# Batch 1's first layer norm as pieces in the queue of keys and values

## The chip, the cores and the metric

The kernel runs on one core of a Trainium2 chip. The core has TensorE (PE; its weight loads are listed as PEld), VectorE (DVE), ScalarE (ACT), GpSimd (POOL) and SyncE (SP), which issues the DMA transfers. Each engine works through its own queue in order, and semaphores tie the queues together. The metric is the device time of one execution in microseconds (us); the figure for a kernel is the median of several runs.

## The reference

The input x has 2 batches of 512 tokens with 512 features, in float32. Four layers are added to x in turn, each of them on a layer norm of x without weights:

```
x = x + attn_a(layernorm(x))   # 32 query heads of 128, 8 key/value heads, causal softmax, rotary positions
x = x + ffn(layernorm(x))      # softmax gate, the best 2 of 8 experts, rank 64
x = x + attn_b(layernorm(x))   # 32 query heads of 16, 8 key/value heads, causal softmax, rotary positions
x = x + ffn(layernorm(x))
```

In attn_a the four weight matrices are stored as integer codes from 0 to 15 with a scale for each group of 128 input rows and each column: w = (code - 8) * scale. The change concerns the very first layer norm, that of attn_a:

```
m = mean(x); v = var(x); (x - m) / sqrt(v + 1e-5)
```

## The kernel before, in words

Everything is tiled to 128 partitions. A batch is NT = 4 tiles of 128 tokens, and the features are NC = 4 chunks of 128.

**The first layer norm.** `two_parts(b)` (L330) does it for batch b through `norm_transposed` (L95). For each of 4 token tiles VectorE takes statistics (L101, L102); ScalarE takes one square root (L104) and VectorE one reciprocal (L106) for all four. Then, tile by tile, VectorE normalizes in place (L110), TensorE transposes the four 128x128 blocks into a PSUM bank (L115, tile pxT_a), and `halves` (L149) splits the result into two parts for the matmuls: ScalarE copies it, rounded, to xh (L151), and VectorE writes the remainder to xl (L152). Both batches are normalized one after the other in the program, batch 0 at L339 and batch 1 at L345, with the loads of the rotary table, of the v scales and of the v codes between them. The scales of the output weights follow (L347). The rows of x lie in two slots of a pool (tag "pT") that the attention later uses for its transposed probabilities.

**Projections.** A head's keys, values or queries are four stages c = 0 to 3 (`projected`, L353). In each, PE multiplies one 128-row chunk of the weights with xh and then with xl into a PSUM bank (L358, L359, tiles ps_k, ps_v, ps_q; two banks, tag "mm"). The first is scaled into SBUF by ScalarE (L363), the other three are scaled and added by VectorE (L365). Keys and queries are then rotated (`rotated`, L369): two VectorE products (L374, L375) and two POOL operations (L376, L377), which write kT or qT. Values are transposed by PE and copied back (L385, L386).

**The attention.** The work is cut into 64 units, one for each of 8 key/value groups g, 2 batches b and 4 heads h, in this order. In step n of the loop at L502, unit n gets its queries, unit n-2 its scores and softmax (L396 matmul, L399 maximum, L404 exponential, L413 division), unit n-3 its weighted values (transposes L424, copies L425, matmuls L429, tile av), and unit n-4 its share of the output projection (L438, L439). These stages are generators, and `in_turn` (L451) takes one piece from each in rotation.

**The queue of keys and values.** Keys and values are made by a further generator, `keys_values(g)` (L476), which for batch 0 and then batch 1 yields 5 pieces for the keys (four stages and the rotation) and 5 for the values. `more` chains those generators over g. Before the loop, 5 pieces are taken (L499), which are the keys of group 0, batch 0. In each step, `some(more, 3 + ...)` (L533) takes 4 pieces while the step's unit is of group 0 (steps 0 to 7), and 3 later. The keys of a unit are read by its softmax two steps after its queries, its values by the weighted values three steps after.

**The order on the engines.** The program's order is a priority, not the order in the queues: an instruction that is ready may be put ahead of earlier ones that are not. The load of the gate weights (L537), which the program issues in step 60 of the loop, stands on SP's queue at 20.86 us.

Of the kernel before, what the change touches and what calls it, by code (L numbers as in the profile page):

```python
# [11 lines left out]
F32 = mybir.dt.float32  # L12
I32 = mybir.dt.int32
F32R = mybir.dt.float32r
AF = mybir.ActivationFunctionType
ALU = mybir.AluOpType
# [3 lines left out]
P = 128  # L20
B, S, DM = 2, 512, 512
NT = S // P
NC = DM // P
# [17 lines left out]
def kernel(  # L41
# [21 lines left out]
    nc = tc.nc  # L63
# [3 lines left out]
    small = ctx.enter_context(tc.tile_pool(name="small", bufs=4))  # L67


    x = {}  # L70
# [7 lines left out]
    ident = const.tile([P, P], F32, tag="ident", name="ident")  # L78
# [7 lines left out]
    eps = const.tile([P, 1], F32, tag="eps", name="eps")  # L86
# [4 lines left out]
    order = const.tile([P, NE], F32, tag="order", name="order")  # L91
    for e in range(NE):
        nc.gpsimd.memset(order[:, e : e + 1], float(NE - e))

    def norm_transposed(b, which, pool, tag, take=None):  # L95


        var = small.tile([P, NT, 2], F32, tag="mv", name=f"mv_{which}_{b}")
        for t in range(NT):
            st = small.tile([P, 6], F32, tag="st", name=f"st_{which}_{b}_{t}")  # L100
            nc.vector.bn_stats(st, x[b, t])  # L101
            nc.vector.bn_aggr(var[:, t, :], st)  # L102
        std = small.tile([P, NT], F32, tag="std", name=f"std_{which}_{b}")
        nc.scalar.activation(std, var[:, :, 1], AF.Sqrt, bias=eps)  # L104
        rstd = small.tile([P, NT], F32, tag="rstd", name=f"rstd_{which}_{b}")
        nc.vector.reciprocal(rstd, std)  # L106
        xT = None if take else xtp.tile([P, NC, S], F32, tag="xnT", name=f"xnT_{which}_{b}")
        for t in range(NT):
            xn = x[b, t] if take else lnp.tile([P, DM], F32, tag="xn", name=f"xn_{which}_{b}_{t}")
            nc.vector.tensor_scalar(  # L110
                xn, x[b, t], var[:, t, 0:1], rstd[:, t : t + 1], ALU.subtract, ALU.mult
            )
            pt = pool.tile([P, NC, P], F32, tag=tag, name=f"pxT_{which}_{b}_{t}")
            for c in range(NC):
                nc.tensor.transpose(pt[:, c, :], xn[:, ts(c, P)], ident)  # L115
            if take:
                take(t, pt)
            else:
                nc.scalar.copy(xT[:, :, ts(t, P)], pt)
        return xT  # L120


    homes, banks, lora = {}, [], {}
# [25 lines left out]
    def halves(src, hi, lo):  # L149

        nc.scalar.copy(hi, src)  # L151
        nc.vector.tensor_tensor(lo, src, hi.bitcast(F32), ALU.subtract)  # L152
# [127 lines left out]
    with ExitStack() as actx:  # L280
# [12 lines left out]
        ps_tp = actx.enter_context(tc.tile_pool(name="ps_tp", bufs=2, space=PSUM))  # L293
# [14 lines left out]
        def whole(codes, u, what, pool=wpool, gpsimd=False):  # L308

            cd = big.tile([P, NC * U], I32, tag="big", name=f"codes_{what}_{u}")  # L310
            nc.sync.dma_start(cd, codes[u])
            w = pool.tile([P, NC, U], F32R, tag="w", name=f"w_{what}_{u}")
            wf = w.rearrange("p c n -> p (c n)")
            if gpsimd:
                nc.gpsimd.tensor_scalar(wf, cd, -8.0, 1.0, ALU.add, ALU.mult)
            else:
                nc.scalar.activation(wf, cd, AF.Copy, bias=-8.0)
            return w

        wkv, xh, xl, own = {}, {}, {}, {}  # L320
# [8 lines left out]

        def two_parts(b):  # L330

            xh[b] = xp.tile([P, NC, S], F32R, tag=f"xh{b}", name=f"xh_{b}")
            xl[b] = xp.tile([P, NC, S], F32R, tag=f"xl{b}", name=f"xl_{b}")
            norm_transposed(
                b, "a", ps_tp, "tp",
                lambda t, pt: halves(pt, xh[b][:, :, ts(t, P)], xl[b][:, :, ts(t, P)]),
            )

        two_parts(0)  # L339

        tab = tabs.tile([P, 2, S], F32, tag="tab", name="tab")
        nc.sync.dma_start(tab, rope_a)
        own["v"] = own_scales(v_scales, 2 * 4 * NC, "v")
        wkv["v"] = whole(v_codes, 0, "v", wkvp, gpsimd=True)
        two_parts(1)  # L345

        so = own_scales(o_scales, A_NH * NC, "o")  # L347

# [20 lines left out]
        def rotated(dst, kind, w, u, h, b, nm):  # L369


            r = yield from projected(kind, w, u, h, b, nm)
            rs = rp.tile([P, S], F32, tag=f"rs{kind}", name=f"rs_{nm}")
            nc.vector.tensor_tensor(rs[0:64], r[64:128], tab[64:128, 1, :], ALU.mult)  # L374
            nc.vector.tensor_tensor(rs[64:128], r[0:64], tab[0:64, 1, :], ALU.mult)  # L375
            nc.gpsimd.tensor_tensor(r, r, tab[:, 0, :], ALU.mult)  # L376
            nc.gpsimd.tensor_tensor(dst, r, rs, ALU.add)  # L377
            yield

        def values_of(dst, w, u, h, b, nm):  # L380

            r = yield from projected("v", w, u, h, b, nm)
            tp = ps_tp.tile([P, NT, P], F32, tag="tp", name=f"tp_{nm}")
            for t in range(NT):
                nc.tensor.transpose(tp[:, t, :], r[:, ts(t, P)], ident)  # L385
            nc.scalar.copy(dst, tp)  # L386
            yield
# [88 lines left out]
        def keys_values(g):  # L476

            u, h = divmod(g, 4)
            if g == 4:
                wkv["k"] = whole(k_codes, u, "k", wkvp)  # L480
                wkv["v"] = whole(v_codes, u, "v", wkvp)
            for b in range(B):
                kTs[g, b] = kvp.tile([P, S], F32, tag="kT", name=f"kT_{g}_{b}")
                vs[g, b] = kvp.tile([P, NT, P], F32, tag="v", name=f"v_{g}_{b}")
                yield from rotated(kTs[g, b], "k", wkv["k"], u, h, b, f"k_{g}_{b}")
                yield from values_of(vs[g, b], wkv["v"], u, h, b, f"v_{g}_{b}")
# [9 lines left out]


        more = keys_values(0)
        in_turn(some(more, 5))  # L499
        units = [(g, b, h) for g in range(A_NKV) for b in range(B) for h in range(A_G)]  # L500
        wo, qTs, prs, ats = {}, {}, {}, {}
        for n in range(len(units) + 4):  # L502
            turn = []

            def at(lag):
                if 0 <= n - lag < len(units):
                    g, b, h = units[n - lag]
                    return (g, b, h, f"{g}_{b}_{h}")

            if at(3):  # L510
                g, b, h, nm = at(3)
# [4 lines left out]
            if at(0):  # L516
                g, b, h, nm = at(0)
                if (b, h) == (0, 0):
                    if g:
                        wq[g] = whole(q_codes, g, "q")  # L520
                    wo[g] = whole(o_codes, g, "o")
                    after = keys_values(g + 1) if g + 1 < A_NKV else iter(())
                    more = chain(more, after)
                qTs[g, b, h] = qtp.tile([P, S], F32, tag="qT", name=f"qT_{nm}")
                turn.append(rotated(qTs[g, b, h], "q", wq[g], g, h, b, f"q_{nm}"))
            if at(4):
                g, b, h, nm = at(4)
                turn.append(output(wo[g], h, g * A_G + h, b, *ats.pop((g, b, h)), nm))
            if at(2):
                g, b, h, nm = at(2)  # L530
# [19 lines left out]
    xtp = ctx.enter_context(tc.tile_pool(name="xnT", bufs=2))  # L550
# [511 lines left out]
```

## Time and profile before

| | |
|---|---|
| median of 3 runs | 1117.19 us (1116.21 to 1117.54) |
| the profiled execution | 1118.06 us, its span 1116.3 us |
| PE busy | 1060.7 us, 4940 matmuls |
| DVE busy | 880.8 us, 2195 instructions |
| ACT busy | 617.4 us, 1421 instructions |
| POOL busy | 587.4 us, 920 instructions |
| L365, scaled sums of the queries | 192 instructions, 747 ns each |
| L115, transposes of the norm, in the first 60 us | 32 instructions, 7.6 us |
| L110, normalizations | 8 instructions, 529 to 1111 ns |

The span is the time from the first to the last instruction of the profiled execution. The page cuts it into 40 slices of 27.9 us and gives for each engine a digit, the busy share in tenths. Other views list the busy time of the engines in any stretch, the chain of work that ended last (each piece led to by what released it), the instructions in order of time, and for one line of the kernel the least, median and longest duration. All times count from the start of the span.

### The profile page before, as it was taken

To read this page: it belongs to the slowest core of one execution; us is meant where nothing else is said; L and a number is where in the kernel's file an instruction comes from. 1 tells how busy PE (TensorE), PEld (TensorE's weight loads), DVE (VectorE), ACT (ScalarE), POOL (GpSimd) and SP (SyncE) were. 2 spreads that over 40 slices of the span, in tenths; PEclk is the share of its full clock that TensorE was granted. 3 is DMA by queue.
4 is the path that set the end of the run, shared out by engine and by line. 5 is a ranking of instruction groups with operands and counts; after the bars stand their busy time and mean duration, and the time that the engine had idled before them with its cause. 6 is when DMAs were issued, how large, how long until landed. Compare 5 with 4: busy or idle time off the path is not lost.

```text
span 1116.3 us, 16200 instructions
## 1 busy us (share of the span) xinstructions
PE 1060.7 (95%) x4940; PEld 708.8 (63%) x4940; DVE 880.8 (79%) x2195; ACT 617.4 (55%) x1421; POOL 587.4 (53%) x920
## 2 busy tenths in 40 slices
PE   5799999999999999999999999999989989999988
PEld 3467677777777777777777777546457555555543
DVE  6889899999999999999999889574376677877252
ACT  3556566577566566566565665513157566585410
POOL 2557566666656656756756666261245566454200
PEclk9999999999999999999999999999989999999999
DMA  7301011022010010010021000042342235111000
GB/s 288 114 1 38 1 38 38 1 76 68 9 39 24 15 38 14 26 38 8 32 76 38 1 1 1 1 156 63 91 156 77 61 106 152 44 44 26 10 33 38
DMA packets 21030, 58.11 MB, mean 52 GB/s; under 512 B 3152, under 2 KB 4112, under 8 KB 18128
## 3 DMA queue, kind: packets, MB, share of 16 engines
q1 hardware_dynamic: 20944, 57.08, 15.6%
q8 instruction: 40, 0.66, 0.2%
q14 instruction: 46, 0.38, 0.1%
HBM read 43.30 MB, written 12.58 MB: 50 GB/s over the span
## 4 chain that ended last, share of the span: by engine, by line
PE 80%; DVE 10%; ACT 3%; POOL 3%; issue 2%; DMA 1%; SPq 0%; ACTq 0%; DVEq 0%; POOLq 0%
PE av L429 11%; PE sc L396 11%; PE tp L424 5%; PE ps_o L439 5%; PE ps_o L438 5%; PE ps_q L358 5%; PE ph_f L207 5%; PE ps_q L359 5%; PE num_b L831 3%; PE st_b L805 3%; PE py_f L266 3%; PE sc_b L758 3%; PE pq_b L678 2%; PE po L885 2%; DVE r_q L365 2%
## 5 line engine op out<-in xcount | busy, mean ns | idle before, releaser
L404 ACT ACTIVATE p<-sc,nmx 128x128 f32<-128x128 f32 (+3 forms) x256 | 135.7, 530 | 95.1 <-DVE nmx L399 92.1
L376 POOL TENSOR_TENSOR r_q<-r_q,tab 128x512 f32<-128x512 f32 x64 | 82.5, 1289 | 190.2 <-DVE rs_q L375 190.2
L396 PE MATMUL sc<-kT,qT 128*128 128x128 f32 (+3 forms) x512 | 180.0, 433 | 1.2 <-POOL qT L377 0.9
L365 DVE SCALAR_TENSOR_TENSOR r_q<-ps_q,s_q,r_q 128x512 f32<-128x512 f32 x192 | 143.4, 747 | 36.1 <-PE ps_q L359 22.4
L413 POOL TENSOR_SCALAR p<-p,rden 128x128 f32<-128x128 f32 (+3 forms) x256 | 140.3, 562 | 58.5 <-DVE rden L411 24.5
L425 ACT COPY pT<-tp 128x128 f32<-128x128 f32 (+3 forms) x256 | 109.4, 428 | 104.1 <-PE tp L424 103.5
L762 DVE CUSTOM_DVE_ANT_0 sc_b<-sc_b,tri 128x128 f32<-128x128 f32 (+3 forms) x256 | 119.6, 516 | 47.3 <-PE sc_b L758 42.5
L429 PE MATMUL av<-pT,v 128*128 128x512 f32 (+3 forms) x512 | 148.5, 433 | 0.0
L429 PEld LDWEIGHTS av<-pT,v 128*128 128x128 f32 x512 | 97.0, 190 | 80.2 <-issue 53.9
L448 DVE SCALAR_TENSOR_TENSOR acc<-ps_o,s_o,acc 128x512 f32<-128x512 f32 x186 | 137.3, 738 | 5.5 <-PE ps_o L439 5.4
L399 DVE CUSTOM_DVE_ANT_0 sc<-sc,tri 128x128 f32<-128x128 f32 (+3 forms) x256 | 125.1, 489 | 8.1 <-PE sc L396 7.3
L358 PE MATMUL ps_q<-xh,w_q 128*128 128x512 f32 x256 | 122.7, 479 | 7.6 <-DVE r_q L365 7.6
L424 PE MATMUL tp<-ident,p 128*128 128x128 f32 x640 | 112.9, 272 | 2.6 <-POOL p L413 2.6
L396 PEld LDWEIGHTS sc<-kT,qT 128*128 128x128 f32 x512 | 95.6, 189 | 25.3 <-ACT p L404 2.0
L438 PE MATMUL ps_o<-ah,w_o 128*128 128x512 f32 x256 | 107.9, 422 | 1.7 <-DVE acc L448 1.0
L811 ACT ACTIVATE pT_b<-st_b 128x384 f32<-128x384 f32 (+1 forms) x192 | 90.1, 528 | 34.4 <-PE st_b L805 33.5
L439 PE MATMUL ps_o<-al,w_o 128*128 128x512 f32 x256 | 104.8, 410 | 3.5 <-DVE al L152 3.5
L424 PEld LDWEIGHTS tp<-ident,p 128*128 128x128 f32 x640 | 83.0, 141 | 30.7 <-issue 6.4
L359 PE MATMUL ps_q<-xl,w_q 128*128 128x512 f32 x256 | 101.2, 395 | 0.0
L814 POOL TENSOR_SCALAR_AFFINE_SELECT pT_b<-pT_b 128x128 f32<-128x128 f32 (+1 forms) x192 | 62.2, 333 | 64.7 <-ACT pT_b L811 62.2
L377 POOL TENSOR_TENSOR qT<-r_q,rs_q 128x512 f32<-128x512 f32 x64 | 85.5, 1335 | 1.0
L446 POOL TENSOR_TENSOR acc<-acc,part 128x512 f32<-128x512 f32 x62 | 79.9, 1288 | 10.2 <-ACT part L445 10.1
(182 smaller groups left out, 2065.4 us busy)
## 6 DMA issues: line engine op xcount, KB each, us to landing
codes_q<-in_q_codes_dram SPq DMA_DIRECT2D x8, 1024.0 KB
codes_o<-in_o_codes_dram SPq DMA_DIRECT2D x8, 1024.0 KB
spread_q<-hl SPq DMA_DIRECT2D x16, 512.0 KB
qs<-spread_q SPq DMA_DIRECT2D x32, 256.0 KB
x_a<-in_x_dram SPq DMA_DIRECT2D x8, 256.0 KB
codes_k<-in_k_codes_dram SPq DMA_DIRECT2D x2, 1024.0 KB
codes_v<-in_v_codes_dram SPq DMA_DIRECT2D x2, 1024.0 KB
x_r<-in_x_dram SPq DMA_DIRECT2D x8, 256.0 KB
```

The costliest lines, as they stand in the source:

```text
L358: nc.tensor.matmul(ps, w[:, c, ts(h, A_HD)], xh[b][:, c, :], start=True, stop=False)
L359: nc.tensor.matmul(ps, w[:, c, ts(h, A_HD)], xl[b][:, c, :], start=False, stop=True)
L365: nc.vector.scalar_tensor_tensor(r, ps, s, r, ALU.mult, ALU.add)
L396: nc.tensor.matmul(sc[:, :n], qT[:, ts(i, P)], kT[:, :n], start=True, stop=True)
L399: nc.vector.tensor_tensor_reduce(sc[:, :n], sc[:, :n], tri[:, S - n :], -(A_HD**-0.5), 3e38, ALU.add, ALU.min, nmx,)
L404: nc.scalar.activation(pr, sc[:, :n], AF.Exp, bias=nmx, scale=-1.0, accum_out=den[:, i % 2 : i % 2 + 1],)
L413: nc.gpsimd.tensor_scalar(prs[j], prs[j], rden[:, j % 2 : j % 2 + 1], 1.0, ALU.mult, ALU.mult)
L424: nc.tensor.transpose(tp[:, j, :], prs[i][:, ts(j, P)], ident)
L429: nc.tensor.matmul(av[:, j * P :], v[:, j, :], pT[:, j, j * P :], start=(j == 0), stop=(j == NT - 1))
L438: nc.tensor.matmul(ps, w[:, h, ts(n, P)], ah, start=True, stop=False)
L439: nc.tensor.matmul(ps, w[:, h, ts(n, P)], al, start=False, stop=True)
L448: nc.vector.scalar_tensor_tensor(to, ps, s, to, ALU.mult, ALU.add)
```

## The change

`norm_transposed` is gone; its body stands in `two_parts`, which is now a generator with five pieces: the statistics of the four tiles with square root and reciprocal, and then one piece for each tile. For batch 0 the generator is run to its end in the old place. For batch 1 it is taken as part of `keys_values(0)`, after the values of batch 0 and ahead of the keys of batch 1. So `more` begins with keys of batch 0 (pieces 1 to 5), values of batch 0 (6 to 10), the norm of batch 1 (11 to 15), keys of batch 1 (16 to 20), values of batch 1 (21 to 25), where the last two were pieces 11 to 15 and 16 to 20. How many pieces a step takes is as before. The instructions, their operands, the pools and the number of buffers are the same.

```diff
-    def norm_transposed(b, which, pool, tag, take=None):
...
         def two_parts(b):
+
             xh[b] = xp.tile([P, NC, S], F32R, tag=f"xh{b}", name=f"xh_{b}")
             xl[b] = xp.tile([P, NC, S], F32R, tag=f"xl{b}", name=f"xl_{b}")
-            norm_transposed(
-                b, "a", ps_tp, "tp",
-                lambda t, pt: halves(pt, xh[b][:, :, ts(t, P)], xl[b][:, :, ts(t, P)]),
-            )
-
-        two_parts(0)
+            var = small.tile([P, NT, 2], F32, tag="mv", name=f"mv_a_{b}")
+            for t in range(NT):
+                st = small.tile([P, 6], F32, tag="st", name=f"st_a_{b}_{t}")
+                nc.vector.bn_stats(st, x[b, t])
+                nc.vector.bn_aggr(var[:, t, :], st)
+            std = small.tile([P, NT], F32, tag="std", name=f"std_a_{b}")
+            nc.scalar.activation(std, var[:, :, 1], AF.Sqrt, bias=eps)
+            rstd = small.tile([P, NT], F32, tag="rstd", name=f"rstd_a_{b}")
+            nc.vector.reciprocal(rstd, std)
+            yield
+            for t in range(NT):
+                xn = x[b, t]
+                nc.vector.tensor_scalar(
+                    xn, xn, var[:, t, 0:1], rstd[:, t : t + 1], ALU.subtract, ALU.mult
+                )
+                pt = ps_tp.tile([P, NC, P], F32, tag="tp", name=f"pxT_a_{b}_{t}")
+                for c in range(NC):
+                    nc.tensor.transpose(pt[:, c, :], xn[:, ts(c, P)], ident)
+                halves(pt, xh[b][:, :, ts(t, P)], xl[b][:, :, ts(t, P)])
+                yield
+
+        for _ in two_parts(0):
+            pass
 
         tab = tabs.tile([P, 2, S], F32, tag="tab", name="tab")
         nc.sync.dma_start(tab, rope_a)
         own["v"] = own_scales(v_scales, 2 * 4 * NC, "v")
         wkv["v"] = whole(v_codes, 0, "v", wkvp, gpsimd=True)
-        two_parts(1)
 
         so = own_scales(o_scales, A_NH * NC, "o")
...
             for b in range(B):
+                if (g, b) == (0, 1):
+                    yield from two_parts(1)
                 kTs[g, b] = kvp.tile([P, S], F32, tag="kT", name=f"kT_{g}_{b}")
```

More of the change, by code (lines that the diff above doesn't have):

```diff
@@ L93 @@
         nc.gpsimd.memset(order[:, e : e + 1], float(NE - e))
-    def norm_transposed(b, which, pool, tag, take=None):
[L98 to L111, printed above, removed]
-            )
[L113 to L120, printed above, removed]
     homes, banks, lora = {}, [], {}
@@ L333, in two_parts @@
             xl[b] = xp.tile([P, NC, S], F32R, tag=f"xl{b}", name=f"xl_{b}")
-            norm_transposed(
-                b, "a", ps_tp, "tp",
-                lambda t, pt: halves(pt, xh[b][:, :, ts(t, P)], xl[b][:, :, ts(t, P)]),
-            )
-        two_parts(0)
+            var = small.tile([P, NT, 2], F32, tag="mv", name=f"mv_a_{b}")
[20 more added lines that the diff above has]
+            pass
         tab = tabs.tile([P, 2, S], F32, tag="tab", name="tab")
```

## The prediction

> **What bounds the kernel now.** I read the page first (busy time, the 40 slices), then stretches of 4 us over the start, then the chain of waits from 17 to 39 us, then the order of VectorE's instructions there.
>
> ```profile
> PE 1060.7 (95%) x4940; PEld 708.8 (63%) x4940; DVE 880.8 (79%) x2195; ACT 617.4 (55%) x1421; POOL 587.4 (53%) x920
> ...
> PE   5799999999999999999999999999989989999988
> ...
> DVE  6889899999999999999999889574376677877252
> ```
>
> TensorE (PE) is busy 95% of the span, and the digits say where it is not: the first two slices, 0 to 56 us. Between 100 and 580 us PE is busy 473.33 of 480.00 us, so a start that is shorter by some time ends the kernel earlier by that time, less the PE work that it left for later. The start itself, by stretches:
>
> ```profile
> core 0: us, PE busy (x) PEld busy (x) DVE busy (x) ACT busy (x) POOL busy (x), PEclk, DMA share, GB/s
> ...
> 24.00:28.00 4.00, 3.87 (x19) 2.96 (x18) 3.44 (x7) 2.54 (x5) 0.00 (x0) 1.00 0.24 70
> 28.00:32.00 4.00, 2.34 (x8) 1.05 (x8) 3.80 (x6) 3.90 (x3) 2.57 (x2) 1.00 0.19 37
> 32.00:36.00 4.00, 3.30 (x14) 1.58 (x12) 3.50 (x6) 2.00 (x3) 0.67 (x1) 1.00 0.99 408
> 36.00:40.00 4.00, 2.58 (x10) 1.57 (x10) 2.39 (x7) 3.81 (x7) 1.87 (x2) 1.00 0.68 236
> ...
> 44.00:48.00 4.00, 2.12 (x9) 1.05 (x9) 3.92 (x7) 0.95 (x2) 3.92 (x5) 1.00 0.00 0
> ```
>
> Here VectorE (DVE) is the fuller engine, except from 36 to 40 us, where it waits for the first rotated queries. From 22.00 to 58.25 us (58.25 is the first weighted-values matmul, av L429) PE is busy 29.01 of 36.25 us and DVE 32.37: 7.24 us of PE time lie idle, 3.88 us of DVE time. The chain of waits (start, length, what) runs through the moved layer norm:
>
> ```profile
> 23.23 1.71 PE pxT_a L115 x8
> ...
> 25.58 1.03 PE pxT_a L115 x4
> 26.64 0.60 ACT xh L151
> ...
> 27.26 0.69 DVE xl L152
> ...
> 27.96 0.69 DVE rs_k L375
> ...
> 28.68 0.69 DVE xl L152
> ...
> 36.68 1.28 POOL qT L377
> ...
> 38.00 0.94 PE sc L396 x4
> ```
>
> All pxT_a, xh and xl after 22 us are batch 1's: 1.71 + 1.03 + 0.60 + 0.69 + 0.69 = 4.72 us of the chain to the first scores at 38.00. None of it is wanted by these scores, which are batch 0's.
>
> **The change part by part.** It adds and removes no instruction. Batch 1's norm is 4 pairs of statistics (0.67 + 0.18 us each), one square root, one reciprocal, 4 normalizations L110, 16 transposes L115, 4 xh copies (0.59) and 4 xl (0.69). It issues no DMA (batch 1's rows are loaded at 4.56 us as before), so SP's queue is passed by nothing, and POOL's neither.
>
> The order on the engines is not the program's (a load that the program issues in step 60, L537, is on SP's queue at 20.86 us). Before, three pairs of statistics stand between 14.86 and 17.05 us, while VectorE has little else that could run. I expect them to stay there, and so the square root at 19.79, ahead of the table load for the first Exp at 37.57: cost zero. If they go later instead, the xl at 17.05 gains about 0.5 us (its xh is there at 16.5), and 4 x 0.85 = 3.4 us fall into fuller time; if the square root lands behind the first Exp, ScalarE reloads twice, 2 x 1.28 = 2.6 us on an engine busy 20.23 of 36.25 us. Bounds: 0.5 gained, 2.6 lost; I take zero, by the nearest row, the gap itself.
>
> What changes is from 21.87 us on:
>
> ```profile
> 21.87 1.91 DVE L110 TENSOR_SCALAR x_a<-x_a,mv_a,rstd_a 128x512 f32<-128x512 f32 x4
> 23.70 0.75 DVE L365 SCALAR_TENSOR_TENSOR r_k<-ps_k,s_k,r_k 128x512 f32<-128x512 f32 x1
> ```
>
> The reader is to see that the last sum of batch 0's keys (23.70; its matmuls end at 22.02) stands behind four normalizations. With these later in priority: r_k at 22.05 to 22.8, its two rs_k (0.69 each) to 24.2. ps_q c0 stays at 22.02; ps_v c0 follows at 22.85 in the bank that r_k frees; ScalarE scales them at 23.3 and 24.0 (0.69 each). ps_q c1 then runs 24.0 to 24.85, and the first of the six L365 for q and v starts at 25.1 rather than 29.29. The six take 4.54 us before (29.29 to 33.83), so they end at about 29.65; rs_q 1.39 and POOL's two with their gaps 2.7 us give first scores at 33.8, against 38.00: 4.2 us. The norm's remains (4 L110, 1.91; 4 xl, 2.76) slip into VectorE's gaps in between, and one L110 too many in front of a waiting L365 costs about 0.5. **First scores 3.7 us earlier**, and, if the steps after it keep their distance, av at 54.5. VectorE's own ledger agrees: by then it has not done batch 1's v (3 L365, 2.25 us), and filling half of its 3.88 idle us gives 1.9: 4.2 us.
>
> Given back: the queue of key/value pieces is five behind. At four a step, batch 1's keys end in step 3 (before: 2), its values in step 4 (before: 3); they are wanted by softmax in step 6 and by the weighted values in step 7, so nothing starves. But batch 1's v (8 matmuls at 0.23 and 4 transposes 0.44 together, by the chain's rows near 56 us) is then PE work in time that PE bounds: 2.3 us. Net **1.4 us, the lower end**.
>
> The upper end is PE's ledger. In the stretch above, PE's idle time from 28 to 32 (1.66) and 36 to 40 us (1.42) is behind the moved work or lacks filler, which the norm now is; that from 44 to 48 (1.88) waits for POOL's probabilities and stays. With both gone 3.1 us. Beyond, 12 of the moved transposes take 1.71 + 1.03 = 2.74 us in the chain, where later groups of four (L424) take 0.44: 1.4 us saved if they run at that later pace. Together 4.5 us. Between 1.4 and 4.5 I take the middle, **3.0 us**, since half of PE's idle time has the norm in front of it in the chain.
>
> Covers: the slot of x_a of batch 1 is wanted by pT of unit 1, first written at 61.19; the norm is done some 20 us earlier. PSUM's two "tp" banks: tp_v ends before 35 us and the first tp of the weighted values is at 46.80, so the transposes find one free; without that cover they wait for one xl, 0.7 us. The transposes of the output scales (L303, 0.42; copy 0.28) pass ahead of the norm; they overtake nothing on the chain but 0.3 us.
>
> [...] The matmul pairs at 21.17 and 21.59 stand 0.43 us apart, those at 48.12 and 48.35 0.23, while the granted clock reads 1.00 in all these stretches: the pace changes near 26 us. [...]
>
> ```profile
> L110 DVE TENSOR_SCALAR x_a<-x_a,mv_a,rstd_a x8: 529/538/1111, 10.5 to 23.2; 128x512 f32<-128x512 f32 x8
> ```
>
> Least, median and longest of L110: the 1111 ns one stands beside POOL's L315 (from 9.39 to 11.29). [...] By the rows alone: 0 to 4 x 0.57 = 2.3 us lost on VectorE; I take 0.5, which is in the sum above.
>
> **Rivals.**
> 1. It washes out, or the order hardly changes. The pieces are ready early, so the norm may be put where it was; or the 2.3 us beside POOL cancel the 1.4 to 3.0. For it: the statistics fill gaps whatever their priority. Against it: at 22.05 a ready L365 has priority now. 1115.0 to 1119.4.
> 2. Slower: a late norm holds PE's queue. Before, the first matmul of batch 1's keys (34.84) comes 5.5 us after the last xl (29.37). Now pieces 15 and 16 are neighbours, and a ps_k that stands in PE's queue ahead of its xl stops everything behind it: L110 0.5 + transposes 0.45 + xh 0.6 + xl 0.7 = 2.3 us, and 1.9 more if a weight conversion (L317, 1.92, three of them from 28 to 37 us) is on ScalarE ahead of xh: 4.2. Less the 1.4 that is sure, 2.8 us slower: 1120.0. It decides once PE waits over some 3.5 us at these lines. Against it: the order puts ready work first.
> 3. A larger gain: all of 4.5, the 0.5 of the statistics, and PE's 1.41 idle us from 72 to 76 (two rs_q of 1.15 and 1.68 beside POOL) drawn apart by the shift: 6.4, so 1110.8.
>
> **How the numbers follow.** The rows are of an execution of 1118.06 us (span 1116.3, 1.8 around it). 1118.06 - 3.0 = 1115.06; that execution is 0.87 above the median of the runs, 1117.19, so I predict 1114.2. Forecast (1.4 to 4.5 faster: 1112.7 to 1115.8) 0.54; washed out or unchanged 0.17; slower 0.23; larger gain 0.06. Over 0.2% (2.2 us, about what a measurement tells from no change) faster: 0.43 of the forecast and the larger gain, 0.49. Within: the forecast's 0.11 and 0.15 of the wash-out, 0.26. Slower: 0.23 and 0.02, 0.25. The range, 1111.0 to 1121.0, takes in the slower rival and leaves out most of the larger gain and stalls that come twice.
>
> **What would show it.** Right: r_k's last L365 near 22 us, first sc near 34 (33 to 35), av near 54.5, batch 1's xl between 26 and 38 us, PE idle from 28 to 40 us down from 3.8 to under 2 us, and PE idle after 100 us unchanged. Wrong: the L110 of batch 1 still ahead of that L365 (rival 1); PE waiting for xl at L358/L359 of ps_k for microseconds (rival 2); L110 over 1 us; a second table load before 50 us; or a first sc that is 4 us earlier with av where it was, which would mean that the start is bound by VectorE's sum of work and not by its order.

## The result and the profile after

The changed kernel takes 1117.65 us (median of 22 runs, 1116.42 to 1120.97); the kernel before, run beside it, 1116.16 us (22 runs: 21 of them from 1113.32 to 1117.95, and one of 1216.47, which the ratio leaves out). The ratio is 1.0019 with an interval of 1.0011 to 1.0027: about 2 us slower, where 3 us faster was forecast. A second set of runs gave 1.0023 (1.0013 to 1.0032). The profiled execution took 1117.18 us, with a span of 1115.4, less than the one shown of the kernel before. After the last copy of weighted values two executions of the kernel before still take 387.3 and 386.2 us, two of the changed one 383.9 and 385.3; the change does not touch that part, so the reading goes by the start and not by the span.

The page of the changed kernel shows how little the totals tell:

```profile
PE 1059.7 (95%) x4940; PEld 708.1 (63%) x4940; DVE 879.9 (79%) x2195; ACT 616.0 (55%) x1421; POOL 586.6 (53%) x920
...
PE   4799999999999999999999999999989989999988
...
DVE  6789899999999999999999889664376677877252
```

The same instructions, and the first digit of PE has fallen from 5 to 4. The stretches of 4 us say where (length, then busy time of PE, PEld, DVE, ACT, POOL, granted clock, DMA):

```profile
core 0: us, PE busy (x) PEld busy (x) DVE busy (x) ACT busy (x) POOL busy (x), PEclk, DMA share, GB/s
24.00:28.00 4.00, 1.81 (x5) 0.80 (x4) 3.97 (x5) 3.65 (x3) 2.62 (x2) 1.00 0.37 88
28.00:32.00 4.00, 3.07 (x6) 1.78 (x7) 3.03 (x5) 0.64 (x1) 0.00 (x0) 0.52 0.92 342
32.00:36.00 4.00, 4.00 (x16) 2.79 (x16) 3.16 (x5) 1.28 (x2) 0.65 (x1) 0.63 0.40 164
...
44.00:48.00 4.00, 1.56 (x8) 1.13 (x9) 2.96 (x8) 1.70 (x6) 2.55 (x4) 1.00 0.80 262
```

From 24 to 28 us PE is busy for 1.81 us, where it was 3.87, while VectorE is full (3.97). In the next two stretches the granted clock is 0.52 and 0.63, where it was 1.00: PE looks full from 32 to 36 us because each matmul is long (L349 0.63 us there, 0.40 at 35.20). What happened at 24 to 29 us stands in the order of the instructions (start, length, engine, line; in brackets the idle time before it and what ended it). L320 is the normalization (L110 before), L355 the scaled sum (L365), L366 and L367 POOL's rotation (L376, L377), L348 and L349 the projections' matmuls (L358, L359):

```profile
24.77 1.29 POOL L366 TENSOR_TENSOR r_k<-r_k,tab 128x512 f32<-128x512 f32 x1 [4.26 <-DVE rs_k L365]
24.92 3.29 DVE L320 TENSOR_SCALAR x_a<-x_a,mv_a,rstd_a 128x512 f32<-128x512 f32 x3
...
25.43 0.40 PE L349 MATMUL ps_v<-xl,w_v 128*128 128x512 f32 x1
26.14 1.33 POOL L367 TENSOR_TENSOR kT<-r_k,rs_k 128x512 f32<-128x512 f32 x1
...
28.13 0.74 DVE L355 SCALAR_TENSOR_TENSOR r_q<-ps_q,s_q,r_q 128x512 f32<-128x512 f32 x1
...
28.93 0.80 PE L348 MATMUL ps_q<-xh,w_q 128*128 128x512 f32 x1 [3.10 <-DVE r_q L355]
```

```profile
L320 DVE TENSOR_SCALAR x_a<-x_a,mv_a,rstd_a x8: 531/537/1491, 10.5 to 27.7; 128x512 f32<-128x512 f32 x8
```

Three normalizations (0.53 to 0.54 us alone) take 3.29 us, since two of them, at 1.42 and 1.49 us, stand beside POOL's rotation of the first keys. The queries' sum that frees PE's bank waits behind them until 28.13, and PE waits 3.10 us for it. The chain of waits (start, length, what) shows what became of the layer norm that had stood in it:

```profile
26.26 1.95 DVE x_a L320 x2
28.21 0.67 DVE r_q L355
28.93 0.80 PE ps_q L348
...
36.71 1.27 POOL qT L367
38.03 0.50 PE sc L386 x2
```

Transposes, xh and xl are out of it, as intended, but two normalizations and slow matmuls are in it, and the first scores come at 38.03, where they came at 38.00. Nothing was gained there.

### The profile page after: what moved, and what is told of

Its sections match the earlier page's. It is cut to its first block, busy times and chain, and to the rows that moved or that the text cites. A ratio compares the mean times of both kernels' runs of the same rounds, so it can differ in the third digit from the quotient of the medians.

```text
span 1115.4 us, 16198 instructions
## 1 busy us (share of the span) xinstructions
PE 1059.7 (95%) x4940; PEld 708.1 (63%) x4940; DVE 879.9 (79%) x2195; ACT 616.0 (55%) x1421; POOL 586.6 (53%) x920
## 4 chain that ended last, share of the span: by engine, by line
PE 80%; DVE 10%; POOL 3%; ACT 3%; issue 2%; DMA 1%; SPq 0%; DVEq 0%; ACTq 0%; POOLq 0%
PE av L419 11%; PE sc L386 10%; PE tp L414 5%; PE ps_o L428 5%; PE ps_o L429 5%; PE ps_q L348 5%; PE ph_f L180 5%; PE ps_q L349 5%; PE py_f L239 4%; PE num_b L823 3%; PE st_b L797 3%; PE sc_b L750 3%; PE pq_b L670 2%; PE po L877 2%; DVE r_q L355 2%
## 5 line engine op out<-in xcount | busy, mean ns | idle before, releaser
L366 POOL TENSOR_TENSOR r_q<-r_q,tab 128x512 f32<-128x512 f32 x64 | 82.8, 1293 | 197.5 <-DVE rs_q L365 197.5
L355 DVE SCALAR_TENSOR_TENSOR r_q<-ps_q,s_q,r_q 128x512 f32<-128x512 f32 x192 | 143.4, 747 | 36.0 <-PE ps_q L349 22.5
L348 PE MATMUL ps_q<-xh,w_q 128*128 128x512 f32 x256 | 124.9, 488 | 8.0 <-DVE r_q L355 7.9
L386 PEld LDWEIGHTS sc<-kT,qT 128*128 128x128 f32 x512 | 95.6, 189 | 25.1 <-POOL qT L367 2.0
L803 ACT ACTIVATE pT_b<-st_b 128x384 f32<-128x384 f32 (+1 forms) x192 | 90.1, 528 | 34.4 <-PE st_b L797 33.5
L349 PE MATMUL ps_q<-xl,w_q 128*128 128x512 f32 x256 | 102.1, 399 | 0.0
L367 POOL TENSOR_TENSOR qT<-r_q,rs_q 128x512 f32<-128x512 f32 x64 | 85.2, 1331 | 0.9
```

Source lines behind the costliest of these rows:

```text
L348: nc.tensor.matmul(ps, w[:, c, ts(h, A_HD)], xh[b][:, c, :], start=True, stop=False)
L349: nc.tensor.matmul(ps, w[:, c, ts(h, A_HD)], xl[b][:, c, :], start=False, stop=True)
L355: nc.vector.scalar_tensor_tensor(r, ps, s, r, ALU.mult, ALU.add)
L386: nc.tensor.matmul(sc[:, :n], qT[:, ts(i, P)], kT[:, :n], start=True, stop=True)
```

## The experiments

Theory A: the three normalizations meet POOL's rotation, PE's queue stands behind them, and the idle time lowers the granted clock afterwards; that eats the gain, and the five pieces that the queue is behind must still be paid. Theory B: the start is bound by the sum of VectorE's work, so the order of the norm does not matter. Further rivals are named in the expectations.

A shift of the start shows in the time less clearly than in the trace, so each run is read by the same marks. All count from the fourth statistics of batch 1, which start at 18.3 to 19.9 us (they follow the arrival of data, which varies): the first scores, the copies of the weighted values of units 0, 8, 24 and 56, in us. Two executions of the kernel before differ by 0.4 in the first scores and by 0.3 from unit 8 on, two of the changed one by 0.8 from unit 0 on.

| kernel | first scores | unit 0 | unit 8 | unit 24 | unit 56 | ratio to before |
|---|---|---|---|---|---|---|
| before | 19.7, 19.3 | 42.4, 42.0 | 131.8, 131.5 | 302.0, 301.7 | 633.4, 633.1 | |
| changed | 19.7, 19.7 | 40.3, 41.1 | 130.4, 131.2 | 304.5, 305.3 | 635.9, 636.6 | 1.0019, 1.0023 |
| norm_early | 17.6 | 38.3 | 128.5 | 302.5 | 633.8 | 0.9994 |
| norm_scalar | 19.5 | 38.0 | 128.6 | 302.7 | 634.2 | 0.9980 |
| five_pieces | 18.9 | 45.6 | 136.2 | 306.4 | 637.8 | 1.0040 |
| before_pool | 22.3 | 46.2 | 135.7 | 305.8 | 637.2 | one run |
| hold | 18.5 | 37.3 | 126.5 | 300.6 | 631.9 | 0.9978 |
| hold_scalar | 15.7 | 36.3 | 125.8 | 300.2 | 631.6 | 0.9970 |
| fill | 19.2 | 38.8 | 128.9 | 302.9 | 634.3 | 0.9993 |
| fill_28 | 18.9 | 37.8 | 127.9 | 301.9 | 633.3 | 0.9988 |
| three | 18.1 | 35.8 | 123.2 | 295.8 | 632.3 | 0.9983 |
| hold_three | 14.8 | 33.3 | 120.9 | 293.6 | 630.9 | 0.9955 |

**norm_early: the normalizations back in front of the keys' last sums, the rest in pieces.** The generator of batch 1 is started in the old place and does statistics and all four normalizations there.

```diff
             nc.vector.reciprocal(rstd, std)
-            yield
             for t in range(NT):
                 ...
                 nc.vector.tensor_scalar(
                     xn, xn, var[:, t, 0:1], rstd[:, t : t + 1], ALU.subtract, ALU.mult
                 )
+            yield
+            for t in range(NT):
...
+        second = two_parts(1)
+        next(second)
```

> All else as in the changed kernel, but batch 1's four normalizations stand where they stood before the change; only its transposes, xh and xl stay in the queue of pieces (an empty piece keeps the count at five). Theory A (in the changed kernel three normalizations meet the two POOL operations that rotate the first keys, take 1.4 us instead of 0.5, and the 3.1 us in which TensorE then waits halve its pace until 34.7 us): the normalizations take 0.6 us or less each, TensorE has no gap over 1.5 us from 22 to 30 us, the granted clock stays 1.00 from 22 to 40 us, the first scores start at 35 to 36 us instead of 38.0, and the last ah starts 2 to 4 us earlier than the 731.5 us of the changed kernel; time 0.1 to 0.3% under the kernel before. Theory B (VectorE's sum of work sets the length of the start, its order is of no account): first scores may move, but the last ah stays within 1 us of 731.5. Theory F (the transposes were the filler that kept TensorE's clock up): the granted clock falls from 22 to 40 us here too, as the transposes are still gone from there.

Measured: ratio 0.9994 (0.9981 to 1.0006), which is not clear of no change; 0.1 to 0.3% less was expected. Batch 1's four normalizations take 0.54 us each, and PE has no gap over 0.7 us between 22 and 30 us. First scores are 2.1 us earlier than in the changed kernel, and unit 8 is 1.9 to 2.7 us earlier. VectorE does the same work here, so its sum alone (theory B) does not decide the start. The last copy of weighted values starts at 731.9 us, within the 1 us of 731.5 that was named for theory B; but the fourth statistics came 1.35 us later in this execution, and counted from them it stands at 712.2, against 713.2 and 713.9 in the changed kernel. The pace is not as clean:

```profile
30.18 0.63 PE L353 MATMUL ps_v<-xl,w_v 128*128 128x512 f32 x1
30.60 0.69 PE L352 MATMUL ps_q<-xh,w_q 128*128 128x512 f32 x1
31.09 0.50 PE L353 MATMUL ps_q<-xl,w_q 128*128 128x512 f32 x1
```

The matmuls of a pair start some 0.43 us apart until 30.6 us, as in the start of the kernel before, though the clock column reads 1.00. Over matmuls that far apart the 1.00 is no reading (the last section has the same in the kernel before), and the run is no evidence on the pace; later, a gap of 2.10 us from 35.2 is followed by 0.53 from 38 us. The missing transposes by themselves (theory F) do not keep the pace down: they are missing in the changed kernel too, and there a pair stands 0.34 us apart at 25.09.

**norm_scalar: the four normalizations on ScalarE.**

```diff
+            if b == 1:
+                off = small.tile([P, NT], F32, tag="off", name="off_a")
+                nc.vector.scalar_tensor_tensor(off, var[:, :, 0], -1.0, rstd, ALU.mult, ALU.mult)
...
-                nc.vector.tensor_scalar(
+                    nc.scalar.activation(
+                        xn, xn, AF.Identity, bias=off[:, t : t + 1], scale=rstd[:, t : t + 1]
+                    )
```

> The changed kernel, but batch 1's four normalizations are done by ScalarE (scale and bias from two small VectorE results) instead of VectorE; transposes, xh, xl and the pieces are as changed. Theory A: nothing of the norm meets POOL on VectorE, so no gap of TensorE over 1.5 us from 22 to 30 us and a granted clock of 1.00 there, first scores at 33.5 to 35 us, the last ah 3 to 5 us before 731.5 us, time 0.2 to 0.4% under the kernel before (1.9 us less VectorE work is part of it). Theory B: only the 1.9 us that leave VectorE show, first scores at 36 us. Theory F: the clock falls from 22 to 40 us all the same.

Measured: ratio 0.9980 (0.9968 to 0.9992). The meeting with POOL is gone (0.80 us each on ScalarE), but the gap is not. It is only led to by another engine:

```profile
25.30 2.92 ACT L324 ACTIVATE x_a<-x_a,off_a,rstd_a 128x512 f32<-128x512 f32 x4
28.12 0.67 ACT L361 ACTIVATE r_v<-ps_v,s_v 128x512 f32<-128x512 f32 x1
```

```profile
28.85 0.79 PE L356 MATMUL ps_v<-xh,w_v 128*128 128x512 f32 x1 [2.66 <-ACT r_v L361]
```

Four ready normalizations stand ahead of the scaling of the first values, which frees PE's other bank; PE idles 2.66 us, the granted clock reads 0.60, 0.50, 0.50 and 0.69 from 28 to 36 us, and the first scores come 19.5 us after the statistics, as in the changed kernel. What theory A expected of this run (no gap over 1.5 us, first scores at 33.5 to 35 us) failed: the gap was 2.66 us, the first scores came at 39.25. So what matters is that ready instructions stand in front of one that PE waits for; POOL only makes them longer (0.54 us to 1.42 and 1.49 in the changed kernel). From unit 0 on this kernel is 1.7 to 3.1 us ahead of the changed one all the same; VectorE has 1.9 us less to do in it, and how much of the lead that is was not parted further.

**five_pieces: the lag of the queue taken away.** One piece more in each of the steps 0 to 4.

```diff
-            turn.append(some(more, 3 + (units[min(n, 63)][0] == 0)))
+            turn.append(some(more, 3 + (units[min(n, 63)][0] == 0) + (n < 5)))
```

> The changed kernel, but five pieces instead of four are taken from the queue of keys and values in steps 0 to 4, so that the five pieces of the norm come on top and group 0's values and all later groups are where they were before the change from step 5 on. The lag theory (the changed kernel loses by having its keys and values five pieces late): the growth of the delay from 0.4 to 2.4 us between units 12 and 24 goes, the last ah starts at 729 to 730 us, and the time is back at that of the kernel before. Theory A: the loss is at 24 to 35 us, which this does not touch; the last ah stays at 731 or above, and the first scores at 38.0.

Measured: ratio 1.0040 (1.0026 to 1.0053), slower than the changed kernel, where the lag theory expected the time of the kernel before. The marks split the lag's price. From unit 8 to unit 24 this kernel takes 170.2 us, as the kernel before does (170.2), and the changed one 174.1: the lag of five pieces costs 3.9 us there. But unit 0 comes 4.5 to 5.3 us later than in the changed kernel: pieces taken in steps 0 to 4 cost more than they do later. A lag is no loss by itself. From unit 2 to unit 63 this kernel stands 4.3 to 4.4 us behind the first profile of the kernel before, by the same marks: in this execution that is the price of the changed order when no piece is postponed.

**before_pool: the meeting with POOL alone, in the kernel before.** Three products, of no use to the result, are put on POOL beside batch 1's normalizations; the buffer they write is allocated earlier.

```diff
         nc.vector.reciprocal(rstd, std)
+        if take and b == 1:
+            for n in range(3):
+                nc.gpsimd.tensor_tensor(
+                    acc[1][:, n, :], tri, rstd[:, 0:1].to_broadcast([P, S]), ALU.mult
+                )
```

> The kernel before, with three POOL products of 128x512 (tri by batch 1's reciprocal) put into a buffer that is overwritten later; they start when that reciprocal is there, near 21 us, so that POOL is busy while VectorE does batch 1's normalizations at 21.87. Theory A, the meeting with POOL by itself: these normalizations take 1.0 to 1.5 us instead of 0.53, the last sum of the keys moves from 23.7 to about 26, and the first scores from 38.0 to 40 or 41 us. Without such a meeting: 0.53 us each and first scores at 38.0.

Measured, in one execution:

```profile
22.07 3.48 POOL L111 TENSOR_TENSOR acc<-tri,rstd_a 128x512 f32<-128x512 f32 x3 [9.72 <-DVE rstd_a L108]
...
22.93 4.93 DVE L117 TENSOR_SCALAR x_a<-x_a,mv_a,rstd_a 128x512 f32<-128x512 f32 x4
...
27.64 0.51 PE L365 MATMUL ps_v<-xh,w_v 128*128 128x512 f32 x1 [1.75 <-POOL w_v L322]
```

Four normalizations take 4.93 us in place of 1.91, by nothing but POOL beside them (0.54, 1.26, 1.26, and 2.11 beside the weight conversion that follows on POOL); first scores are 2.6 to 3.0 us later, unit 8 some 4 us, and the granted clock falls to 0.71 and 0.50 between 28 and 32 us. The three products also push POOL's conversion of the value weights (L322, which starts at 25.64, behind them), so 1.75 us of PE's wait is not the meeting; the run shows the lengthening cleanly and its price only as an upper bound.

**before_again and after_again: both kernels once more, as they are.**

> The kernel before once more, to see how far the marks of the start repeat from one execution to the next: fourth statistics of batch 1 between 18.3 and 19.8 us (by when the first codes land), first scores 19.5 to 20 us after it, last ah 710 to 712 us after it. If the marks after the statistics differ by over 1 us, differences of that size between single profiles say nothing.

> The changed kernel once more, timed beside the kernels of this call on one chip: 0.1 to 0.3% above the kernel before; the three normalizations beside POOL's first rotation 1.4 us twice, TensorE's gap of about 3 us and the lower granted clock after it again; last ah 713 us after the fourth statistics.

Measured: both come back as they were. The changed kernel shows 0.54, 1.41, 1.49 and 0.54 us, a gap of 3.33 us, and a clock of 0.61, 0.50, 0.50 and 0.68 from 28 to 36 us; the kernel before 0.54 four times, no gap over 1.6 us, and 1.00 from 28 to 36 us. The reading of the first trace is no accident of one execution. One thing differs: a later wait of the changed kernel (2.47 and 2.48 us, for POOL's probabilities) is followed by a clock of 1.00 in the first execution and by 0.73 and 0.50 from 48 to 52 us in the second, whose unit 0 is 0.8 us later.

**hold: the normalizations later.** The reciprocal of batch 1 is made to depend on batch 0's first values by adding zero times them, so that no normalization is ready before the six sums.

```diff
+            if b == 1:
+                nc.vector.scalar_tensor_tensor(
+                    rstd, held["v"][:, :NT], 0.0, rstd, ALU.mult, ALU.add
+                )
             yield
```

> The changed kernel, but batch 1's normalizations can only start when the first values are summed (its reciprocal gets zero times these values added), which is after the six sums of the first queries and values. Theory A (the normalizations between the first keys and the first queries, prolonged by POOL, make TensorE's gap, and the gap halves its pace): no gap over 1.5 us from 20 to 32 us after the start, first scores 14.5 to 16.5 us after the fourth statistics (19.7 in the changed kernel), last ah 1.5 to 4 us nearer to it than in the changed kernel (713.2), time 0.15 to 0.4% under the changed kernel. Rival: the meeting only moves on to POOL's rotation of the first queries, normalizations of 1.4 us again, first scores 18 us or more after the fourth statistics, and time as changed. Theory B (sum of work): time as changed.

Measured: ratio 0.9978 (0.9969 to 0.9987). The first queries' sum starts at 25.77 and the six end at 30.73 (28.13 and 33.86 in the changed kernel). But the meeting has only moved, to POOL's rotation of the queries:

```profile
32.23 1.26 POOL L372 TENSOR_TENSOR r_q<-r_q,tab 128x512 f32<-128x512 f32 x1 [4.83 <-DVE rs_q L371]
33.57 1.33 POOL L373 TENSOR_TENSOR qT<-r_q,rs_q 128x512 f32<-128x512 f32 x1
```

Beside these, two normalizations take 1.39 and 1.49 us, PE idles 2.01 us, and the clock falls again (0.91, 0.50, 0.74 from 32 to 38 us). The first scores, 18.5 us after the statistics, are where the rival put them (18 or more) and only 1.2 us earlier than in the changed kernel; unit 8 is 3.9 to 4.7 us earlier, and the time is not as in the changed kernel, as the rival had it.

**hold_scalar: the same with the normalizations on ScalarE** (both edits above).

> As the held one, with the four normalizations on ScalarE. They then neither meet POOL nor stand in front of the values' first scaling, which made a gap of 2.7 us and halved the pace in the run with ScalarE alone. Theory A: first scores 14 to 15.5 us after the fourth statistics, no granted clock under 1.00 from 27 to 36 us, last ah 2 to 4 us nearer to the fourth statistics than in the changed kernel, time 0.2 to 0.5% under the changed kernel and 0 to 0.3% under the kernel before. If the clock has no part (only work on VectorE counts): no better than the run with ScalarE alone, 0.1 to 0.2% under the kernel before.

Measured: ratio 0.9970 (0.9960 to 0.9981); first scores 15.7 us after the statistics (14 to 15.5 expected), 4.0 earlier than in the changed kernel. That is the size that the prediction gave this step (3.7), now that nothing ready stands in front of the sums and nothing meets POOL. A gap of 2.5 us remains in front of the first scores, and the clock reads 0.54 and 0.61 from 36 to 40 us.

**fill and fill_28: PE's gap filled with work of no use.** After the first stage of batch 0's values, 16 or 28 transposes of a tile that is there, their results unread.

```diff
                     nc.scalar.activation(r, ps, AF.Copy, scale=s)
+                    if nm == "v_0_0":
+                        spare = ps_o.tile([P, NT, P], F32, tag="o", name="spare")
+                        for m in range(28):
+                            nc.tensor.transpose(spare[:, m % 4, :], r[:, ts(m % 4, P)], ident)
```

> The changed kernel with 16 spare transposes on TensorE, of the first values' first scaling, whose result nobody reads. They stand in TensorE's queue ahead of the matmuls of the values' second stage, and so in the gap of 3.1 us; VectorE's order is that of the changed kernel, and its three normalizations meet POOL as before. If the gap halves TensorE's pace, and this pace is a part of the loss: matmul pairs of queries and values 0.23 us apart from 28 to 34 us after the start instead of 0.43, first scores 18.2 to 18.9 us after the fourth statistics instead of 19.7, the last units' ah about 1 us nearer to them, time 0.05 to 0.15% under the changed kernel although it does 1.7 to 3.4 us more work. If the pace has no part, only VectorE's 1.9 us: first scores at 19.7 or later.

> The changed kernel with 28 spare transposes (12 more than in the run with 16) on TensorE between the first and the second stage of batch 0's values; their results are not read, and they are extra work. The sixteen ended at about 28.1 us there and left 1.85 us of TensorE idle, and the granted clock still fell to 0.50 from 31.5 to 35 us. Twenty-eight, at 0.12 us each, are to reach to about 29.5 us, so that the idle time before the second stage of the queries is under 0.7 us. VectorE is as in the changed kernel (three normalizations of 0.53, 1.41 and 1.49 us). Theory A (the idle time is what lowers TensorE's pace): no stretch at 0.50 between 28 and 38 us, the six sums of queries and values take 4.5 to 4.8 us instead of 5.2 to 5.7, and first scores come 17.7 to 18.9 us after batch 1's statistics (changed kernel 19.67 to 19.69). Rival (the lower pace follows from something else, such as the time since the start or the kind of the instructions): the clock falls to 0.50 again in that stretch, sums 5.2 us or more, first scores 19.2 or later. The time of the kernel: 1116 to 1118.5.

Measured: 16 transposes, ratio 0.9993 (0.9979 to 1.0007). They end at 28.1 us and 1.85 us of idle time stay; the clock is 1.00 until 30 us and 0.50 from 32 to 34. First scores come 19.2 us after the statistics, between the 18.2 to 18.9 and the 19.7 that were named for the two answers: that run leaves the question open. With 28, ratio 0.9988 (0.9976 to 0.9999), the largest gap there is 0.45 us. Its stretches of 4 us:

```profile
core 0: us, PE busy (x) PEld busy (x) DVE busy (x) ACT busy (x) POOL busy (x), PEclk, DMA share, GB/s
...
28.00:32.00 4.00, 3.55 (x20) 2.25 (x18) 3.24 (x6) 0.99 (x1) 0.00 (x0) 1.00 0.94 299
32.00:36.00 4.00, 3.45 (x18) 2.18 (x17) 3.69 (x6) 2.36 (x2) 0.78 (x1) 1.00 0.58 225
```

The clock is 1.00 where the changed kernel has 0.52 and 0.63, with the same three normalizations (0.54, 1.42, 1.50 us, ending at 28.57). So it is the idle time that the low clock went with here: 0.50 after a wait of 3.10 us, 1.00 from 28 to 36 us where the largest gap is 0.45. Unit 8 comes 2.5 to 3.3 us earlier than in the changed kernel: a kernel with 28 transposes more is quicker. Three of the numbers expected were missed: the time, 1115.18 us, is under the 1116 named, first scores are at 18.93 (just above 18.9), and the six sums take 5.24 us (28.49 to 33.73), since the second waits 0.59 us for matmuls that stand behind the transposes. The last five take 3.91 us, against 5.07 in the changed kernel (28.79 to 33.86): 1.2 us of the pace's price lie there, and the rest comes between the first scores and unit 0, where it was not parted further.

**three and hold_three: fewer pieces at the start.** Three pieces in every step, in the changed kernel and in hold_scalar.

```diff
-            turn.append(some(more, 3 + (units[min(n, 63)][0] == 0)))
+            turn.append(some(more, 3))
```

> The changed kernel with three pieces in all steps. Same question without the hold: if early pieces cost, 0.05 to 0.25% under the changed kernel (which is 0.2% above the kernel before); if only the meeting with POOL and the pace count, as the changed kernel.

> The held kernel with normalizations on ScalarE, and three pieces of the queue of keys and values in all steps (four in steps 0 to 7 before); batch 1's keys then end in step 4 and its values in step 6, one step ahead of their use. If pieces taken early cost (five more of them in steps 0 to 4 made the changed kernel slower by about 0.3%), because the start is short of VectorE and the later steps have room: the first ah 1 to 2 us earlier than the 36.3 us after the fourth statistics, time 0.05 to 0.2% under the held one. If the pieces are only given back later, as in the changed kernel: time within 0.1% of the held one (0.30% under the kernel before).

Measured: ratios 0.9983 (0.9968 to 0.9997) and 0.9955 (0.9941 to 0.9969; 1112.91 against 1117.96 us). At unit 8 the first is 7.2 to 8.0 us ahead of the changed kernel; by unit 56 3.6 to 4.3 us of it are left, the rest went back into pieces taken later. hold_three is the quickest kernel of all, and has no gap of PE over 0.64 us between 19 and 60 us. That the lead isn't given back whole fits five_pieces: early pieces cost more than late ones. Both runs gained more than expected: by the two ratios to the kernel before, the first lies 0.36 to 0.40% under the changed kernel (0.05 to 0.25 expected), and hold_three's unit 0 comes 3.0 us before hold_scalar's (1 to 2 expected). Why by so much isn't settled. Three pieces a step in the kernel before was not run, so whether this gain needs the moved norm at all is not shown.

The last column follows the marks at unit 56 loosely: most kernels are another 1 to 3 us better in time than there, which was not followed up.

## Why the prediction was wrong, point by point

- **Statistics stay, cost zero: right.** They stand from 14.87 to 19.2 us, the square root at 19.80, the reciprocal at 21.89, and there is no second table load.
- **The keys' sum moves ahead of the normalizations: right.** r_k's last sum is at 22.08 (22.05 predicted, 23.70 before), ps_q c0 at 22.03, ps_q c1 at 24.12 (24.0 predicted).
- **"First scores 3.7 us earlier": the step that failed.** It rests on "one L110 too many in front of a waiting L365 costs about 0.5", which was to hold the meeting with POOL as well. In place of one of 0.5 us stood three of 3.29 us together. One normalization was expected at a time, in the gaps; but all four are ready at once at 22.1; one went ahead of rs_k, and the other three ahead of the first of the six sums, whose matmuls end only at 25.07. That sum started at 28.13 and not at 25.1: 3.0 us. About 1.5 of them are the three at their plain length, and 1.8 (0.88 + 0.95) POOL's part, less a little that had been in the estimate's slack. Then the six sums took 5.7 us (28.13 to 33.86) and not 4.54: 1.2 us, the slow pace, for which the prediction's sum has no term. Together 4.2 us, which is the whole 4.2 worked out before the 0.5 was taken off.
- **"Av at 54.5": hit, by luck.** The first weighted-values matmul came at 54.52 (58.25 before), but not by way of the first scores, which had not moved, and in the second executions it stands at 56.73, against 58.83. By its av VectorE had done two sums of batch 1's keys in the changed kernel; in the kernel before it had done all three, their two rs_k and the three sums of the values. The lead goes with work put off, and by unit 24 it is given back.
- **The meeting with POOL was sized too low.** The rows' upper end, 4 x 0.57 = 2.3 us, was near; 0.5 was taken. The meeting came early, with POOL's rotation of the first keys. POOL's two, the first of them started ahead of the normalization (24.77 and 24.92 us), take 1.29 and 1.33 us (1.27 and 1.29 in the kernel before), and two of VectorE's grow from 0.54 to 1.42 and 1.49.
- **The pace of PE: no term of the sum, and the one that decided.** The faster pace was there ahead of the wait: the pair at 25.09 us stands 0.34 us apart. It was lost again, for the q and v pairs fill PE only while VectorE frees their banks, here to 25.83 us. After the wait of 3.10 us the matmuls are slow from 28.9 to about 34.7 us. Its price, by fill_28 at unit 8, is 2.5 to 3.3 us, where the prediction's sum has nothing. By the marks this one term turns the sign: without it the kernel stands level with the kernel before at units 24 and 56 (301.9 and 633.3 against 301.7 to 302.0 and 633.1 to 633.4).
- **Given back, 2.3 us: the mechanism right, the size not.** From unit 8 to unit 24 every kernel with the lag of five and four pieces a step takes 174.0 to 174.4 us against 170.2: 3.8 to 4.2 us. The jump of some 2 us at units 20 to 24, where the old queue has run dry and the new one still hands out three a step, was the part foreseen; the other 1.8 comes before it, by unit 19.
- **PE's ledger, up to 4.5 us: not had.** Idle PE from 28 to 40 us fell from 3.78 to 2.45 us, but from 24 to 28 us it rose from 0.13 to 2.19, and the wait for POOL's probabilities stayed (2.44 us idle from 44 to 48, 1.88 before).
- **The rivals.** The slower case was foreseen with the wrong mechanism: no ps_k waited for its xl. What held PE's queue was a sum behind a ready normalization on VectorE. The signs named for "wrong" did say it: L110 over 1 us. One row was misread on the way, without weight in the sum: from 24 to 28 us PE (3.87) was the fuller engine before the change, not VectorE (3.44).

The sum that the runs support at unit 56: 4.2 us that the changed order would be worth at the first scores (hold_scalar reached 4.0) did not come, and what lead remained at unit 8 (0.3 to 1.4 us) stands against 3.9 us given back: 2.5 to 3.6 us later by this, 2.5 to 3.5 by the marks, 2.1 and 2.6 by the two ratios.

## What to carry to other kernels

Work made "lower in priority" that became ready all at once still went in front of what was not ready at that moment (three normalizations, 3.29 us, ahead of a sum whose matmuls ended at 25.07), so before counting a gain ask what the first waiting instruction of the bound engine will find ahead of it, and how long that takes with its neighbours running. A wait on TensorE can cost more than its length: after the one of 3.10 us here the matmuls were slow, at 2.5 to 3.3 us on top of it. And where the piece goes and how many are taken early are two questions: with the norm held until the first values are done and done on ScalarE the same idea gives 0.9970, with three pieces a step besides 0.9955.

## What the runs showed of the hardware

- The granted clock read 0.50 after most of the longer waits of TensorE at the start. In the changed kernel it reads 0.50 from 28.16 to 34.99 us, about a wait of 3.10 us that ends at 28.93. After 3.33 us in after_again and 2.66 in norm_scalar it reads 0.50 from 30 to 34 us, after 2.50 in hold_scalar 0.54 from 36 to 38, after 2.10 in norm_early 0.53 from 38 to 40, after 2.01 in hold 0.50 from 34 to 36, after 1.85 in fill 0.50 from 32 to 34, after 1.75 in before_pool 0.50 from 30 to 32. After 1.48 us in the kernel before (to 30.08) and with no gap over 0.45 us in fill_28 (25 to 36 us) it reads 1.00 from 28 to 36 us. The length of the wait alone does not decide: 2.48 us (45.16 to 47.64 in after_again) were followed by 0.73 and 0.50 from 48 to 52 us, 2.47 us (43.76 to 46.23 in the changed kernel) by 1.00, and a PE that is idle throughout 36 to 38 us in five_pieces by 1.00 from 38 to 44. What parts these was not shown.
- The column of the granted clock can read 1.00 while matmuls are 0.43 us apart, against 0.23 later: at the start of the first profiled execution of the kernel before, and in norm_early until 30.6 us. In the first of these the trace's record of the clock begins only at 26.46 us, and the column shows 1.00 where it has no entry; in the other execution of the kernel before the column reads 0.50 from 20 to 26 us. The distance of the matmuls is the safer reading.
- One form of instruction has many lengths: the normalization takes 0.53 to 0.54 us alone, 1.26 to 1.50 beside one POOL product, 1.09 to 1.11 beside the end of POOL's weight conversion of 1.90 us (batch 0's first, in both kernels), and 2.11 beside one of 1.95 us (before_pool).
